# Keys and values lead the queries by eight tiles in the last layer, and the first new rows are gathered inside the projection

## The chip, the cores and the metric

The kernel runs on one core of a Trainium2 chip. The metric is the device time of one execution in microseconds (us), and a smaller time is better. Each engine of the core (TensorE or PE for matrix products, VectorE or DVE, ScalarE or ACT, GpSimd or POOL, and SyncE or SP, which issues transfers) takes its own list of instructions in order and waits for the others through semaphores.

## The reference

Four layers add to a residual x of 2048 tokens by 512 features. The first three (mixtures of experts, attention with low-rank projections, soft routing) are not touched. The last layer matters here:

```
# _L3_cond_ref, cut: new keys and values go into a paged cache, then window attention
q = x @ Wq.T; k = x @ Wk.T; v = x @ Wv.T     # 8 query heads, 4 key heads, 64 wide
q = _rms(q, q_norm_scale); k = _rms(k, k_norm_scale)
pos = kv_lens[:, None] + arange(Tx)
q = _rope(q, pos); k = _rope(k, pos)
k_blocks = k_blocks.at[blk, :, off, :].set(k)                 # and the same for v
allowed = (kpos <= pos) & (kpos > pos - 256)
p = softmax(where(allowed, q @ k_all.T / 16, -inf))
y = (p @ v_all) @ Wo.T
# _L3_ffn_ref: y is quantised to int8 by row, multiplied with an int8 weight, scaled, bias added
```

For each of the 32 sequences a window of the cache is attended to. Some of its rows are old (they come from the given cache), some are new (keys and values of this layer, from whichever sequence wrote to that block of the cache).

## The kernel before, in words

`layer3` works on 16 tiles of 128 tokens (`NT` = 16) in two stages.

**Projection.** A list `units` holds (1, i) for "keys and values of tile i" and (0, i) for "queries of tile i". It is built with `LAG` = 5: the queries of tile t − 5 follow the keys and values of tile t. So five key-and-value units come first, then the two kinds alternate, and after (1, 15) a few query units remain. The last `LAST` = 3 query tiles (13, 14, 15) are not in the list. The loop over u runs through the units and five steps more. In each step:

- `turn` transposes a tile of x on PE for the next kv unit and keeps the result for LAG + 3 = 8 tiles, since the queries use it later;
- four matmuls (L1852) multiply the tile with the weights into PSUM (`pp`);
- `l3_length` squares (ACT L1947), sums (DVE L1949) and takes the power −1/2 (POOL L1952);
- two steps later (one for the last kv tile) `l3_rotate` multiplies with the norm (DVE `n` L1964), with the cosine table (DVE `tc` L1970) and with the sine table (POOL `ts` L1970); one step after that its `add` (DVE L1979) finishes the rotation;
- a finished kv tile is stored to the DRAM buffer `newkv` (SP, L1879); a finished query tile is transposed five steps after its unit by `heads` (PE L1826, two ACT copies L1828 into `qT`);
- from u = 3 to 26 `old_rows` loads one of the first 24 cache tiles `kvt` from the old cache.

Query tiles i ≥ NT − LAG = 11 are `late`: they are only copied to `qlate` (ACT L1860) and normalised and rotated during attention, by the generator `queries`.

After the loop `new_rows(0)` and `new_rows(1)` gather new rows over the old ones: three indirect transfers each (POOL L284), which read `newkv` and so wait until all its stores have landed. They are kept in program order against one another.

**Attention.** A loop over s works in steps of one sequence and half of its heads: `keys` (PE transposes `kp` L2003, ACT copy `kT`), `scores` (PE `sp`, DVE, ACT exponential), `turn0`/`turn1` (PE `pT`), `values` (PE `op`), `product` (PE `y`). Its first steps also project the tiles 13 to 15 (`project`, PE L1910, ACT copy L1912) and call `new_rows(2)`, `new_rows(3)` and so on. A scheduler merges the instructions of the program into one list for each engine; only those that are pinned or kept in program order among themselves are not moved against one another.

Of the kernel before, what the change touches and what calls it, by code (L numbers as in the profile page):

```python
# [22 lines left out]
NT = B * T // P  # L23
# [1724 lines left out]
            yield  # L1748


LAG = 5
LAST = 3


def layer3(g, w, xs, xb):
# [3 lines left out]
    with ExitStack() as ctx:  # L1759
# [6 lines left out]
        def fetch(i):  # L1766
            if i < NT:
                x[i] = g.load_x(xp, xs, i, 4, later=True)
# [11 lines left out]
        def old_rows():  # L1780

            if not kvs or len(kvs[-1]) == 3:
                if len(kvs) == B:
                    return
                kvs.append([])
            t = cache.tile([CH, D], F32, name="kvt")
            g.dma(t, w["rows"][len(kvs) - 1, len(kvs[-1])])
            kvs[-1].append(t)

        def new_rows(b):  # L1790
            if b < B:
                for c in range(3):
                    col = c * B + b
                    g.gather(kvs[b][c], new, w["oidx"][0:CH, col : col + 1], bound=N - 1, later=True)

        with ExitStack() as c1:
            xp = c1.enter_context(tc.tile_pool(name="l3x", bufs=4, reuse_waits="tile"))
            for part in (slice(0, 4), slice(4, NT)):
                g.dma(tab[1][:, part], w["tab"][:, 1, part])
                fetch(2 if part.start == 0 else 3)  # L1800
            sb = c1.enter_context(tc.tile_pool(name="l3pj", bufs=2, reuse_waits="tile"))
            ps = c1.enter_context(tc.tile_pool(name="l3pq", bufs=3, space=PSUM, reuse_waits="tile"))
            units = [
                (z, i) for t in range(NT + LAG) for z, i in ((1, t), (0, t - LAG)) if 0 <= i < NT - (not z) * LAST
            ]

            lag = [1 if unit == (1, NT - 1) else 2 for unit in units]
            xT, held, turned = {}, [], {}

            def turn(i):  # L1810
                if i < NT - LAST:
                    xT[i] = g.transpose4(ps, sb, x[i], "xT3", bufs=3, keep=LAG + 3, pin=True)
                elif i < NT:

                    tp = ps.tile([P, 4, P], F32, name="tp", tag="tp", bufs=3)
                    for c in range(4):
                        g.first(c, nc.tensor.transpose(tp[:, c, :], x[i][:, c * P : (c + 1) * P], g.ident))
                    j = 4 * (i - NT + LAST)
                    xT[i] = tab[1][:, j : j + 4, :]
                    g.evac(xT[i], tp)  # L1820
                fetch(i + 4)

            def heads(ps, i, q):
                tp = ps.tile([P, 4, P], F32, name="tp", tag="tp", bufs=3)
                for c in range(4):
                    nc.tensor.transpose(tp[:, c, :], q[:, c * P : (c + 1) * P], g.ident)  # L1826
                for b in range(2):
                    nc.scalar.copy(  # L1828
                        qT[i][:, b], tp[:, :, 64 * b : 64 * b + 64].rearrange("p (a h) t -> p a h t", a=2)
                    )  # L1830

            slow = []
            turn(0)
            outs = []
            for u in range(len(units) + 5):
                if u == 1:
                    g.dma(wq, a["w_q3"])
                    g.dma(tab[0], w["tab"][:, 0])
                elif u == 12:
                    w["w_o3"] = g.load(wp, "w_o3", later=True)  # L1840
                    w["jt"] = g.load(wp, "jt", later=True)
                    for k in ("wqT", "wsb"):
                        t = wp.tile(list(w[k].shape), w[k].dtype, name=f"{k}3")
                        g.dma(t, w[k])
                        w[k] = t
                if u < len(units):
                    z, i = units[u]
                    if z:
                        turn(i + 1)
                    pp = ps.tile([P, D], F32, name="pp3", tag="pp", bufs=5)  # L1850
                    for c in range(4):
                        nc.tensor.matmul(  # L1852
                            pp, xT[i][:, c, :], (w["w_kv3"] if z else wq)[:, c, :], start=c == 0, stop=c == 3
                        )
                    late = not z and i >= NT - LAG
                    out = wp.tile([P, D], F32, name=f"qlate{i}") if late else sb.tile([P, D], F32, name="qkv3", bufs=6)
                    outs.append(out)
                    if late:

                        nc.scalar.copy(out, pp)  # L1860
                        slow.append((i, out))
                        held.append(None)
                    elif z:
                        nc.scalar.copy(out[:, 256:512], pp[:, 256:512])
                        held.append((pp, out, l3_length(g, sb, pp[:, 0:256])))
                    else:
                        held.append((pp, out, l3_length(g, sb, pp)))
                for k, (z, i) in enumerate(units[: u + 1]):
                    if not held[k]:
                        continue  # L1870
                    if u == k + lag[k]:
                        pp, out, r = held[k]
                        held[k] = l3_rotate(
                            g, sb, out[:, 0:256] if z else out, pp[:, 0:256] if z else pp, r, tab[z][:, i]
                        )
                    elif u == k + lag[k] + 1:
                        out = held[k]()
                        if z:
                            nc.sync.dma_start(out=new[i * P : (i + 1) * P, :], in_=outs[k])  # L1879
                        else:  # L1880
                            turned[k] = out
                if 3 <= u < 27:
                    old_rows()
                if u - 5 in turned:
                    heads(ps, units[u - 5][1], turned[u - 5])
            new_rows(0)
            new_rows(1)

        sb = pool("l3sb", 2)
        ps = pool("l3ps", 3, space=PSUM)  # L1890
# [51 lines left out]
def l3_length(g, sb, src, late=False):  # L1942

    nc = g.nc
    m = src.shape[1] // 64
    sq = sb.tile([P, m, 64], F32, name="sq3")
    nc.scalar.activation(sq, src.rearrange("p (h d) -> p h d", d=64), AF.Square)  # L1947
    ss = sb.tile([P, m], F32, name="ss3", bufs=3)
    nc.vector.tensor_reduce(ss, sq, AX.X, ALU.add)  # L1949
    nc.vector.tensor_scalar(ss, ss, 1.0 / 64, 1e-6, ALU.mult, ALU.add)  # L1950
    r = sb.tile([P, m], F32, name="r3", bufs=3)
    ins = nc.gpsimd.tensor_tensor(r, ss, g.c("nhalf")[:, 0:m], ALU.pow)  # L1952
    if late:
        g.pin(ins)
    return r


def l3_rotate(g, sb, out, src, r, tab):


    nc = g.nc
    m = src.shape[1] // 64
    n = sb.tile([P, m, 64], F32, name="n3")
    g.tc.keep_in_program_order(nc.vector.tensor_tensor(  # L1964
        n, src.rearrange("p (h d) -> p h d", d=64), r.unsqueeze(2).to_broadcast([P, m, 64]), ALU.mult
    ))
    tc_ = sb.tile([P, m, 2, 32], F32, name="tc3")
    ts = sb.tile([P, m, 2, 32], F32, name="ts3")
    for t, k, eng in ((ts, 1, nc.gpsimd), (tc_, 0, nc.vector)):
        eng.tensor_tensor(  # L1970
            t.rearrange("p h z d -> p h (z d)"), n,
            tab[:, 64 * k : 64 * k + 64].unsqueeze(1).to_broadcast([P, m, 64]), ALU.mult,
        )

    def add():
        o = out.rearrange("p (h z d) -> p h z d", z=2, d=32)
        for z, op in ((0, ALU.subtract), (1, ALU.add)):
            g.tc.keep_in_program_order(
                nc.vector.tensor_tensor(o[:, :, z, :], tc_[:, :, z, :], ts[:, :, 1 - z, :], op)  # L1979
            )  # L1980
        return out

    return add
# [178 lines left out]
```

## Time and profile before

| | us |
|---|---|
| median of three runs | 2708.14 (2706.84 to 2720.64) |
| the profiled execution | 2699.47 |
| its span in the trace | 2697.7 |
| mean granted TensorE clock | 0.969 of full |
| projection of the last layer | about 2284 to 2392 |
| attention at an even pace | from about 2434 |

How to read the profile: the page counts the busy time of each engine and the costliest groups of instructions by line, output and input. The timeline lists instructions of all engines by start, with length, engine, line, operation, output and input; in square brackets stands how long the engine had been idle before, and what ended this. The windows give the busy time of each engine in a stretch, with the number of instructions, the granted clock, the share of the transfer engines and what they moved in GB/s. The view of waits sums idle time by the instruction that waited and by what released it.

### The profile page before, as it was taken

To read this page: it belongs to the slowest core of one execution; us is meant where nothing else is said; L and a number is where in the kernel's file an instruction comes from. 1 tells how busy PE (TensorE), PEld (TensorE's weight loads), DVE (VectorE), ACT (ScalarE), POOL (GpSimd) and SP (SyncE) were. 2 spreads that over 40 slices of the span, in tenths; PEclk is the share of its full clock that TensorE was granted. 3 is DMA by queue.
4 is the path that set the end of the run, shared out by engine and by line. 5 is a ranking of instruction groups with operands and counts; after the bars stand their busy time and mean duration, and the time that the engine had idled before them with its cause. 6 is when DMAs were issued, how large, how long until landed. Compare 5 with 4: busy or idle time off the path is not lost.

```text
span 2697.7 us, 42340 instructions
## 1 busy us (share of the span) xinstructions
PE 2526.4 (94%) x16523; PEld 1623.4 (60%) x16523; DVE 1416.6 (53%) x3439; ACT 723.6 (27%) x1501; POOL 850.8 (32%) x904
## 2 busy tenths in 40 slices
PE   6999998996699999996899999999999999989998
PEld 5777775563565555564566666666666665435554
DVE  4666655643744444444444444555554431557886
ACT  2344430111311121010222222222222221236664
POOL 2222214623232233212222333233332321563440
PEclk9999999997699999997899999999999999999999
DMA  2333214445656976544222222222222222523441
GB/s 98 131 123 116 90 70 169 158 151 196 214 181 226 339 260 227 201 163 169 59 69 69 73 81 82 74 73 72 73 73 76 80 71 99 182 77 108 136 138 48
DMA packets 136213, 343.58 MB, mean 127 GB/s; under 512 B 24249, under 2 KB 25049, under 8 KB 128704
## 3 DMA queue, kind: packets, MB, share of 16 engines
q1 hardware_dynamic: 100368, 245.84, 26.4%
q0 software_dynamic: 35056, 89.13, 11.0%
q10 hardware_dynamic: 576, 5.77, 0.5%
q8 instruction: 134, 2.20, 0.3%
q14 instruction: 79, 0.65, 0.1%
HBM read 247.10 MB, written 109.58 MB: 132 GB/s over the span
## 4 chain that ended last, share of the span: by engine, by line
PE 43%; DVE 8%; issue 1%; DMA 1%; ACT 0%; POOL 0%; another core or an unknown queue 0%; SPq 0%; ACTq 0%; POOLq 0%; DVEq 0%
PE out L1539 8%; PE lp L1396 7%; PE pp L1852 3%; PE gp L1528 3%; PE zp L1473 3%; PE y L2099 2%; PE yp L1341 2%; PE op L2077 2%; PE pT L2052 2%; PE hp L1505 2%; PE sp L2030 2%; DVE xt L1025 1%; PE ep L1482 1%; DVE inv L1432 1%; PE kp L2003 1%
## 5 line engine op out<-in xcount | busy, mean ns | idle before, releaser
L943 PE MATMUL gu<-xT,wt 128*128 128x320 f32 x1472 | 407.8, 433 | 0.0
L943 PEld LDWEIGHTS gu<-xT,wt 128*128 128x128 f32 x1472 | 278.2, 191 | 123.1 <-issue 16.2
L1539 PE MATMUL out<-sb_w,gT 128*128 128x512 f32 x512 | 233.6, 599 | 11.1 <-DVE nn L1376 6.7
L1396 PEld LDWEIGHTS lp<-xnT,sb_mu 128*128 128x128 f32 x2048 | 236.1, 194 | 8.7 <-issue 6.7
L962 PE MATMUL y<-wt,hT 128*128 128x512 f32 (+1 forms) x552 | 239.4, 605 | 1.2 <-DVE yo L971 0.7
L1396 PE MATMUL lp<-xnT,sb_mu 128*128 128x128 f32 x2048 | 239.1, 277 | 1.5 <-DVE xnT L256 0.8
L1473 PE MATMUL zp<-sb_w,xnT 128*128 128x512 f32 x512 | 228.3, 595 | 2.7 <-DVE z L1475 2.6
L284 POOL DMA_INDIRECT kvst<-kv,gidx x96 | 96.8, 1009 | 264.4 <-DMA oldkv<-kvst 190.3
L1532 DVE COPY gT<-gp 128x512 f32<-128x512 f32 x64 | 44.3, 691 | 248.4 <-PE gp L1528 248.0
L1539 PEld LDWEIGHTS out<-sb_w,gT 128*128 128x128 f32 x512 | 93.4, 190 | 116.2 <-issue 95.2
L1473 PEld LDWEIGHTS zp<-sb_w,xnT 128*128 128x128 f32 x512 | 93.7, 190 | 110.5 <-issue 97.4
L284 POOL DMA_INDIRECT xr<-rows,stok x115 | 110.1, 957 | 150.2 <-PE tp L924 79.7
L962 PEld LDWEIGHTS y<-wt,hT 128*128 128x128 f32 (+1 forms) x552 | 80.3, 171 | 99.7 <-issue 83.1
L284 POOL DMA_INDIRECT kvt<-newkv,oidx x96 | 98.0, 1021 | 131.9 <-DMA kvt<-oldkv 99.1
L677 POOL TENSOR_TENSOR ga<-ga,sg 128x320 f32<-128x320 f32 x64 | 55.2, 862 | 265.5 <-ACT sg L673 265.5
L284 POOL DMA_INDIRECT yk<-ys,slot x96 | 97.6, 1016 | 126.3 <-SPq L823 65.3
L1510 ACT ACTIVATE h<-hp 128x512 f32<-128x512 f32 x128 | 69.5, 594 | 222.2 <-PE hp L1505 222.1
L673 ACT ACTIVATE sg<-ga 128x320 f32<-128x320 f32 x64 | 30.0, 469 | 277.1 <-DVE ga L671 271.1
L924 PEld LDWEIGHTS tp<-sb_cst,xr 128*128 128x128 f32 x460 | 53.5, 146 | 66.0 <-issue 40.1
L971 DVE TENSOR_TENSOR yo<-y,bd 128x512 f32<-128x512 f32 (+1 forms) x96 | 66.3, 690 | 50.8 <-PE y L962 47.2
L1434 POOL TENSOR_TENSOR eT<-eT,inv 128x512 f32<-128x512 f32 x64 | 71.9, 1125 | 64.9 <-DVE inv L1433 59.5
L1401 DVE TENSOR_TENSOR lT<-lp,cmu 128x512 f32<-128x512 f32 x64 | 43.5, 680 | 92.3 <-PE lp L1396 86.2
(379 smaller groups left out, 4558.1 us busy)
## 6 DMA issues: line engine op xcount, KB each, us to landing
wt<-w_e SPq DMA_DIRECT2D x32, 1538.0 KB
ys<-yo SPq DMA_DIRECT2D x115, 256.0 KB
oldkv<-kvst SPq DMA_DIRECT2D x96, 224.0 KB
kvt<-oldkv SPq DMA_DIRECT2D x96, 224.0 KB
ys<-zero SPq DMA_DIRECT2D x10, 2048.0 KB
xt<-x SPq DMA_DIRECT2D x62, 256.0 KB
x<-xt SPq DMA_DIRECT2D x48, 256.0 KB
wt<-w_e SPq DMA_DIRECT2D x7, 1536.0 KB
```

Source lines behind the costliest of these rows:

```text
L284: ins = self.nc.gpsimd.indirect_dma_start(out=out, out_offset=None, in_=src, in_offset=bass.IndirectOffsetOnAxis(ap=idx, axis=0), **kw)
L677: nc.gpsimd.tensor_tensor(ga, ga, sg, ALU.mult)
L943: nc.tensor.matmul(o, wj[:, c, ic * P : (ic + 1) * P], xT[:, c, :], start=c == 0, stop=c == 3)
L962: nc.tensor.matmul(y[row : row + n, :], hTs[u][:, ic, col : col + n], wd[:, ic, :], start=ic == 0, stop=ic == 1,)
L971: nc.vector.tensor_tensor(yo[r], y[r], bd[r], ALU.add)
L1396: g.first(e + c, nc.tensor.matmul(lp[:, e, :], w["mu"][:, c, (4 * q + e) * P : (4 * q + e + 1) * P], self.xnT[:, c, :], start=c == 0, stop ...
L1434: g.pin(nc.gpsimd.tensor_tensor(e3, e3, inv.unsqueeze(2).to_broadcast([P, 8, T]), ALU.mult))
L1473: g.first(c, nc.tensor.matmul(zp, self.xnT[:, c, :], w["w1"][:, c, cols], start=c == 0, stop=c == 3))
L1510: g.pin(nc.scalar.activation(self.hs[q][b], hp[:, b], AF.Gelu))
L1528: g.first(e + b + k, nc.tensor.matmul(gp[r, e, cols], self.hs[q][b][:, e, r], self.lT[q][:, e, cols], start=True, stop=True))
L1539: g.first(e, nc.tensor.matmul(self.out, self.gTs[q][:, e, :], w["w2"][:, 4 * q + e, :], start=q + e == 0, stop=q + e == 6 and q == 3))
L1852: nc.tensor.matmul(pp, xT[i][:, c, :], (w["w_kv3"] if z else wq)[:, c, :], start=c == 0, stop=c == 3)
```

## The change

The queries now follow the keys and values at a distance of eight tiles. The transposed x tiles are kept for 11 tiles instead of 8, because `keep` is LAG + 3. A constant of its own, `LATE` = 5, keeps the set of late query tiles as it was (11 and 12 in the list). The list has 29 units as before; the unit (1, 15) is number 22 in it instead of 25. The calls of `new_rows(0)` and `new_rows(1)`, which stood after the loop, now stand in the loop, three and four steps after that unit, which is u = 25 and u = 26. `new_rows(2)` and the following ones are called where they were.

```diff
-LAG = 5
+LAG = 8
+LATE = 5
 LAST = 3
...
-                    late = not z and i >= NT - LAG
+                    late = not z and i >= NT - LATE
...
                 if 3 <= u < 27:
                     old_rows()
+
+                if u - units.index((1, NT - 1)) in (3, 4):
+                    new_rows(u - units.index((1, NT - 1)) - 3)
                 if u - 5 in turned:
                     heads(ps, units[u - 5][1], turned[u - 5])
-            new_rows(0)
-            new_rows(1)
```

## The prediction

> **What bounds the kernel now.** I read four views, in this order: the page (who is busy), the windows around the stage the change touches, the timeline of its end, and the waits there.
>
> ```profile
> PE 2526.4 (94%) x16523; PEld 1623.4 (60%) x16523; DVE 1416.6 (53%) x3439; ACT 723.6 (27%) x1501; POOL 850.8 (32%) x904
> ...
> L284 POOL DMA_INDIRECT kvt<-newkv,oidx x96 | 98.0, 1021 | 131.9 <-DMA kvt<-oldkv 99.1
> ```
>
> TensorE is busy 94% of the span, so a change that only moves work can gain only where it stands still. The 96 gathers that fetch new rows cost POOL about 1 us each, a tenth of its busy time. Next the windows (us, then busy time of PE, PEld, DVE, ACT, POOL, then the clock):
>
> ```profile
> 2300.00:2350.00 50.00, 50.00 (x147) 24.07 (x147) 30.46 (x83) 11.25 (x29) 29.17 (x27) 1.00 0.54 185
> 2350.00:2400.00 50.00, 47.76 (x141) 23.16 (x140) 31.98 (x79) 16.82 (x43) 32.49 (x29) 0.97 0.33 108
> 2400.00:2425.00 25.00, 14.54 (x56) 6.89 (x55) 7.24 (x25) 9.51 (x21) 19.61 (x20) 0.89 0.17 44
> 2425.00:2450.00 25.00, 24.28 (x160) 14.33 (x162) 19.07 (x70) 16.23 (x49) 9.11 (x9) 0.84 0.27 74
> ```
>
> The projection is solid TensorE until about 2392; the hole is the passage into attention, where PE is busy 14.5 of 25 us. The timeline shows what fills the passage:
>
> ```profile
> 2377.68 3.60 PE L1852 MATMUL pp<-w_kv,tab 128*128 128x512 f32 x8
> ...
> 2388.86 3.60 PE L1852 MATMUL pp<-w_q,xT 128*128 128x512 f32 x8
> ...
> 2391.62 0.34 SPq L1879 DMA_DIRECT2D newkv<-qkv  x1
> ...
> 2392.31 1.27 POOL L1970 TENSOR_TENSOR ts<-n,tab 128x512 f32<-128x512 f32 x1 [1.76 <-DVE n L1964]
> ...
> 2394.43 1.22 POOL L284 DMA_INDIRECT kvt<-newkv,oidx  x1 [0.85 <-DMA xt<-x2b]
> ...
> 2395.13 0.73 PE L1826 MATMUL tp<-sb_cst,qkv 128*128 128x128 f32 x4 [2.24 <-DVE qkv L1979]
> 2395.65 5.24 PE L1910 MATMUL pp<-w_q,tab 128*128 128x512 f32 x8
> ...
> 2404.43 0.32 PE L2003 MATMUL kp<-sb_cst,kvt 112*128 112x112 f32 x1 [1.25 <-DMA kvt<-newkv,oidx]
> ...
> 2417.66 1.67 POOL L1952 TENSOR_TENSOR r<-ss,sb_cst 128x8 f32<-128x8 f32 x1
> ...
> 2421.92 0.82 PE L2003 MATMUL kp<-sb_cst,kvt 112*128 112x112 f32 x3 [7.48 <-ACT qlate L1912]
> ...
> 2434.22 0.51 PE L2003 MATMUL kp<-sb_cst,kvt 112*128 112x112 f32 x3
> ```
>
> The last key-and-value tile (kv15) is multiplied at 2377.68, its rows are stored at 2391.62, the first gather follows 2.8 us later, and eighteen gathers at one per 1.28 us hold POOL to 2417.6. The power (L1952) of query 11 stands behind them. The waits of 2390 to 2432 give its price:
>
> ```profile
> PE kp L2003 <- ACT qlate L1912: 7.5, 1, 7.5
> ...
> DVE ss L1949 <- POOL r L1952: 6.7, 1, 6.7
> ...
> PE kp L2003 <- DMA kvt<-newkv,oidx: 1.8, 2, 1.2
> ```
>
> The gathers' landing, which the change brings forward, cost PE only 1.8 us; their occupation of POOL costs more: DVE stops 6.7 us and PE 7.5 us.
>
> **What the Trainium skill says.** "TensorE: Matmul & The Clock Gate", What's actually happening: the array runs at half or full clock, watched in windows of about 3.4 us; an idle window halves it. The trace agrees: granted clock is 0.5 from 2395.5 to 2398.9 and from 2419.4 to 2433.1, and eight matmuls that take 3.60 us take 5.24 at 2395.65. The same page (Architectural detail) calls the GpSimd queue strict first in, first out; the trace agrees, query 11's power starting only after gather eighteen. "DMA: Bandwidth & Descriptors", Anatomy of one DMA: about 2 us fixed, mostly the receipt of the write. The trace has 2.8 us from the store's issue to the gather; I use 2.8.
>
> **The change part by part.** In the compiled order the instructions are the same ones; only places differ.
>
> *Where kv15 goes.* After it come six query units instead of three. A query unit takes 3.44 us on PE, a head's transposes 0.44. Query 12 ends at 2391.4 (before 2392.3: two transposes now stand after it). So kv15 ends at 2391.4 − 6×3.44 − 3×0.44 = 2369.5, instead of 2381.1. Store after the same 10.6 us: 2380.1; first gather 2.8 later: 2382.95, 11.5 us earlier. SP issues the stores in order, each just when its tile is ready, and the x loads were issued at least 10 us ahead, so neither queue pays. The other end of the stage (eight kv units ahead instead of five) is costed at nothing: a kv unit needs of POOL 1.12+0.88 us and of DVE about 2, under PE's 3.9. If an x tile came late there, PE would wait for it; three tiles brought forward by 3.4 us each bound that at 10 us.
>
> *POOL's new order.* This is what the diff doesn't show. Only six gathers are written into the loop, but the scheduler lets later ones pass the queries' rotations (ts, 1.27 us) too: gather, power q9, gather, ts q7, 3 gathers, power q10, gather, ts q8, 3 gathers, ts q9, 2 gathers, ts q10, 7 gathers, power q11, 6 gathers. With 1.28 per gather, 1.64 per power and 1.27 per ts, from 2382.95: ts q7 ends 2388.4, ts q8 2396.5, ts q9 2401.7, ts q10 2405.5, gather eighteen 2414.4, power q11 2416.1, the last gather 2423.7 (before 2427.0). Before, ts q10 ended 2393.6, ahead of every gather.
>
> *What that does to PE.* PE is in order and each head's transposes wait for ts plus DVE's add (0.76). The transposes of q8, q9, q10 come at 2397.3, 2402.5, 2406.4 instead of 2388.4, 2392.3, 2395.1. Project13 stands behind them: 2406.9 instead of 2395.65, **11.2 us later**. PE is nearly idle from 2392 to 2406, so the clock is halved and project13 takes 5.24 again, to about 2412.4.
>
> *What is given back.* Before, the stretch from the end of project13 (2400.9) to the kp of 2421.92 took 21.0 us. Gone from it are (a) the two gather waits, 1.8, since the first nine rows land early; (b) the stall on query 11's power, 7.5: it is ready at 2416.1, while DVE needs it only after project14 (2414.4 to 2417.9) and the copy and square of its result (0.6 each), at about 2419. ACT has one square more than before behind the last head copy (six masks and two late queries, 4.3 us, until 2412.5); the first key copy then comes at once, beside project14: nothing. So this kp comes at 2412.4 + 21.0 − 9.3 = 2424.1, 2.2 late. (c) The idle of 2414 to 2422 brought the half clock of 2419.4 to 2433.1, under which two attention steps took 2434.22 − 2421.92 = 12.3 us. Without the idle they run at full clock. From 2434.22 on such a step takes 3.67 us with the output product beside it; these two have none yet. PE was busy 10.3 of the 12.3 us, which is 5.2 at full clock, and two steps of 3.67 are 7.3; I take 5.8 to 6.8. The kp of 2434.22 thus comes at 2429.9 to 2430.9. **Net: 3.4 to 4.3 us earlier, I take 4.** From there the loop is the same work at its own pace.
>
> The profiled execution took 2699.47 us with a span of 2697.7; it becomes 2695.5. The median of the runs is 2708.14, 8.7 above the profiled one; I carry the difference over: **2704 us**.
>
> Unknown costs, from both sides: gathers beside DVE work, 1.22 (the first) to 1.5 us, which for the ten before ts q10 means −0.6 to +2.2; the two steps after it 5.2 to 12.3 (taken 6.3), that is −1 to +6; project13 at full clock −1.6, at half 0 (taken); key copies behind ACT's squares 0 (taken) to +1.5; an x tile late at the start 0 (taken) to +10.
>
> **Rivals.** *Forecast:* delay 11 us, returned in the passage: 2704.
> *Faster:* POOL gets through the mixed order sooner (the heads late by about 5 us instead of 11) and PE stays warm. The passage holds 21.3 us of PE work at full clock in 41.9 us, so 20.6 is all that can be won; with 5 us lost (the six gathers written into the loop, 7.7, less POOL's slack of 1.0 per query unit over three units) kp comes at 2392.3+21.3+5 = 2418.6, 15.6 earlier: 2692.5. For it: first gather 11.5 us earlier and the power stall gone. Against it: ten gathers stand ahead of ts q10, 12.8 us that cannot be overlapped in a first-in queue.
> *Slower:* the heads of q8 to q10 wait behind gathers and the old stall isn't returned, only moved: with before's 38.6 us from project13 to kp at 2434.22 unchanged, the end is 2406.9+38.6 = 2445.5, 11.3 later; each microsecond that ts q10 is later than 2405.5 adds one. With gathers at 1.5 (+2.2) and ACT's +1.5 it is +15: 2723. It decides when ts q10 ends after 2407.7 and DVE still waits for query 11's power. For it: every link is in order. Against it: the power has 3 us to spare.
> *Gathers don't move in effect:* the first gather waits for all stores and an older load (0.85 <-DMA xt in before); if this keeps it at 2394, ts q7 to q10 stand behind that wait too and project13 is later by up to 11.5 us more: 2704 + 11.5 = 2715, a loss with the same sign as the slower rival. Against it: the loads concerned were issued long before.
>
> **How the numbers follow.** What a measurement of this kernel can tell from no change is 0.5%, 13.5 us. Forecast 0.62 (its own range 2695 to 2715), faster rival 0.14, slower 0.17, late gather 0.07. The range takes in the forecast's bounds and part of both sides: 2690 to 2722. Faster than 2694.6: 0.15. Slower than 2721.7: 0.20. Between: 0.65.
>
> **What would show it.** First gather near 2383; ts q10 (POOL L1970) near 2404 to 2406; PE idle before the transposes at L1826 about 4 to 6 us each for q8 and q9, 3 for q10; project13 at 2406 to 2408 at half clock; no wait of DVE ss on POOL r; the 7.5 us of kp on qlate gone; clock full by 2420. Wrong, if PE shows no idle before L1826 (then faster), or if a wait of 6 us or more stands after 2412 (then slower).

## The result and the profile after

On the chip of the prediction the changed kernel took 2703.29 us (median of 14 runs, 2695.53 to 2717.24) against 2711.03 us before (14 runs, 2706.23 to 2720.64). The ratio is 0.9973, 95% interval 0.9962 to 0.9983: about 7 us less, where the prediction had called anything under 13.5 us no change.

The time of a whole run hides where this came from, so times below are also given against the start of the last layer's projection, its first key-and-value matmul; "+127" means 127 us after it. In the profiled run of before this start is at 2281.87, after it is at 2288.09: everything ahead of it, which the change doesn't touch, took 6.2 us longer in the second execution. That is why the profiled execution after has a span of 2703.5 us and yet no slower last layer.

First the windows of the changed kernel (us, busy time of PE, PEld, DVE, ACT, POOL, clock, share of the transfer engines, GB/s):

```profile
2350.00:2400.00 50.00, 48.23 (x140) 22.91 (x138) 29.77 (x73) 12.57 (x33) 34.28 (x28) 1.00 0.29 91
2400.00:2425.00 25.00, 12.64 (x39) 6.83 (x40) 9.07 (x21) 8.48 (x20) 21.31 (x19) 0.66 0.27 69
2425.00:2450.00 25.00, 25.00 (x168) 14.09 (x168) 19.92 (x78) 20.32 (x59) 9.97 (x10) 1.00 0.27 76
```

The hole is about as large as before (12.6 busy us of 25, before 14.5), but it lies earlier in the stage, which stands 6.2 us later in this trace. Its clock is lower (0.66, before 0.89), and the stretch after it is full at full clock (25.00 busy, clock 1.00; before 24.28 at 0.84). Next the timeline of TensorE and POOL in the hole (start, length, engine, line, operation; in brackets the idle time before it and its end):

```profile
2389.51 1.40 POOL L284 DMA_INDIRECT kvt<-newkv,oidx  x1 [2.36 <-DMA kvt<-oldkv]
...
2402.36 1.27 POOL L1972 TENSOR_TENSOR ts<-n,tab 128x512 f32<-128x512 f32 x1
...
2404.57 1.09 PE L1827 MATMUL tp<-sb_cst,qkv 128*128 128x128 f32 x4 [6.34 <-DVE qkv L1981]
...
2410.11 1.09 PE L1827 MATMUL tp<-sb_cst,qkv 128*128 128x128 f32 x4 [4.46 <-DVE qkv L1981]
...
2412.16 1.28 POOL L1972 TENSOR_TENSOR ts<-n,tab 128x512 f32<-128x512 f32 x1
...
2414.38 1.08 PE L1827 MATMUL tp<-sb_cst,qkv 128*128 128x128 f32 x4 [3.18 <-DVE qkv L1981]
2415.26 5.57 PE L1912 MATMUL pp<-w_q,tab 128*128 128x512 f32 x8
...
2422.51 1.67 POOL L1954 TENSOR_TENSOR r<-ss,sb_cst 128x8 f32<-128x8 f32 x1
...
2437.97 0.51 PE L2005 MATMUL kp<-sb_cst,kvt 112*128 112x112 f32 x3
```

The three heads of q8, q9 and q10 wait 6.34, 4.46 and 3.18 us, 14.0 in sum, each for DVE's add, and this for a sine product (POOL L1972) that stands among gathers. Project13 starts at 2415.26, which is +127.2 (before +113.8), at half clock. From there nothing stalls. The waits from 2370 to 2440 say it in one view:

```profile
DVE qkv L1981 <- POOL ts L1972: 15.2, 4, 6.4
PE tp L1827 <- DVE qkv L1981: 14.0, 3, 6.3
...
POOL kvt L284 <- DMA kvt<-oldkv: 2.4, 1, 2.4
```

No line "DVE ss <- POOL r" and no "PE kp <- ACT qlate" is left in this stretch; they were 6.7 and 7.5 us. The seventh key transposes, which ended the passage before at 2434.22 (+152.35), come at 2437.97 (+149.88), 2.5 us earlier.

### The profile page after: what moved, and what is told of

Read it like the earlier page. It is cut to its first block, busy times and chain, and to the rows that moved or that the text cites. A ratio compares the mean times of both kernels' runs of the same rounds, so it can differ in the third digit from the quotient of the medians.

```text
span 2703.5 us, 42331 instructions
## 1 busy us (share of the span) xinstructions
PE 2524.2 (93%) x16508; PEld 1622.9 (60%) x16523; DVE 1416.7 (52%) x3439; ACT 721.4 (27%) x1501; POOL 854.1 (32%) x904
## 4 chain that ended last, share of the span: by engine, by line
PE 42%; DVE 9%; issue 1%; POOL 1%; DMA 1%; ACT 0%; another core or an unknown queue 0%; SPq 0%; ACTq 0%; POOLq 0%; DVEq 0%
PE out L1539 8%; PE lp L1396 7%; PE gp L1528 3%; PE zp L1473 3%; PE pp L1853 3%; PE yp L1341 2%; PE y L2101 2%; PE hp L1505 2%; PE op L2079 2%; PE pT L2054 2%; PE sp L2032 2%; DVE xt L1025 1%; PE ep L1482 1%; DVE inv L1432 1%; PE kp L2005 1%
## 5 line engine op out<-in xcount | busy, mean ns | idle before, releaser
L284 POOL DMA_INDIRECT yk<-ys,slot x96 | 98.6, 1027 | 125.4 <-DVE adf L1159 65.2
```

The source lines that it names most:

```text
L284: ins = self.nc.gpsimd.indirect_dma_start(out=out, out_offset=None, in_=src, in_offset=bass.IndirectOffsetOnAxis(ap=idx, axis=0), **kw)
```

## The experiments

They ran on three more occasions, each with runs of the kernel before on the same chip (three different chips). Its median was 2660.7 us in the first (e1 to e4), 2712.7 in the second (e5 to e8) and 2659.5 in the third (e9 to e12); it had been 2711.0 at the prediction. There are thus two groups of chips, about 50 us apart, and this turned out to matter. Each of the three was used on one occasion only, so the runs don't tell a matter of the chip from one of the occasion; where the text says chip, it can be either. Positions against the stage's start, from one profiled execution each:

| kernel | chip, before's median | ratio to before (95%) | project13 | seventh keys | last output |
|---|---|---|---|---|---|
| before | 2711 | 1 | +113.8 | +152.4 | +412.4 |
| changed | 2711 | 0.9973 (0.9962 to 0.9983) | +127.2 | +149.9 | +412.0 |
| e1 gathers only | 2661 | 1.0002 (0.9993 to 1.0011) | +114.3 | +146.5 | +404.0 |
| e2 lead only | 2661 | 1.0011 (1.0003 to 1.0019) | +127.1 | +150.0 | +406.1 |
| e3 before, six buffers | 2661 | 0.9966 (0.9954 to 0.9978) | +114.3 | +140.5 | +394.0 |
| e4 later gathers held back | 2661 | 1.0005 (0.9997 to 1.0013) | +123.9 | +148.0 | +405.6 |
| e5 changed again | 2713 | 0.9985 (0.9976 to 0.9994) | +127.2 | +149.7 | +413.4 |
| e6 sines on VectorE | 2713 | 0.9989 (0.9979 to 1.0000) | +117.6 | +150.4 | +414.7 |
| e7 changed, six buffers | 2713 | 0.9965 (0.9952 to 0.9978) | +127.2 | +150.4 | +412.0 |
| e8 before, six buffers, early projections | 2713 | 1.0002 (0.9989 to 1.0015) | in the loop | +155.4 | +420.4 |
| e9 before again | 2660 | 1.0004 (0.9994 to 1.0013) | +114.3 | +146.2 | +403.7 |
| e10 lead of six, six buffers | 2660 | 0.9967 (0.9955 to 0.9980) | +116.0 | +139.4 | +394.5 |
| e11 sines on VectorE, six buffers | 2660 | 0.9976 (0.9967 to 0.9985) | +117.5 | +140.3 | +394.3 |
| e12 as e3 | 2660 | 0.9966 (0.9953 to 0.9979) | +113.8 | +138.5 | +392.6 |

**e1 and e2: the two halves of the change.** Against the changed kernel, e1 takes the lead back and e2 the early call of the gathers:

```diff
 e1
-LAG = 8
+LAG = 5
 e2
-                if u - units.index((1, NT - 1)) in (3, 4):
-                    new_rows(u - units.index((1, NT - 1)) - 3)
...
+            new_rows(0)
+            new_rows(1)
```

> LAG stays 5; only the first two groups of gathers are called inside the loop, three and four steps after the last key-and-value unit. If the change works through the order of the units (theory A), this alone does nothing: ratio to before 0.999 to 1.001, passage from the end of query 12 to the seventh key transposes about 42 us as before, first gather right after query 10's rotation, 18 gathers in a row, the 7 us stop of DVE on query 11's power still there. If the early call of the gathers is what brings the gain (theory B), ratio about 0.997 and the passage is shorter by 2 us or more.

> LAG 8 with LATE 5, but the gathers called after the loop as before. Theory A: the same as the changed kernel, ratio to before about 0.997, first gather about 11 us earlier against the stage's start, heads of q8 to q10 late by 4 to 6 us each, passage about 40 us. Theory B: no gain, ratio 0.999 to 1.001.

Measured: 1.0002 and 1.0011. In the compiled program every engine's list of e1 equals that of before, instruction by instruction, and e2's equals that of the changed kernel: the scheduler put the gathers in the same places, whichever of the two steps of the program called them. So the half of the change that moves the calls does nothing, and theory B is out: what is left is the lead of eight tiles. The positions of e2 are the changed kernel's through the whole passage (+101.4 for the first gather, waits of 6.34, 4.46 and 3.18 us, the seventh keys at +150.0 where the changed kernel had +149.9). But its ratio isn't: on this chip the same lists are 0.1% slower than before. The difference is on before's side. Here its passage is 5.9 us shorter (seventh keys at +146.5 instead of +152.4), so that the same changed passage is 2.5 us shorter than before's on one chip and 3.5 us longer on the other. The seventh keys of e1 and e2, whose stages start at 2252.47 and 2256.82:

```profile
2398.97 0.51 PE L2005 MATMUL kp<-sb_cst,kvt 112*128 112x112 f32 x3
...
2406.79 0.51 PE L2004 MATMUL kp<-sb_cst,kvt 112*128 112x112 f32 x3
```

At the last output 2.1 of the 3.5 us are left in the pair of traces; the medians of e2 and of before on this chip differ by 3.6 us (2664.26 and 2660.70).

**e3: the wait on query 11's power.**

```diff
-    ss = sb.tile([P, m], F32, name="ss3", bufs=3)
+    ss = sb.tile([P, m], F32, name="ss3", bufs=6 if late else 3)
...
-    r = sb.tile([P, m], F32, name="r3", bufs=3)
+    r = sb.tile([P, m], F32, name="r3", bufs=6 if late else 3)
```

> The kernel before, with six instead of three buffers for the sums and powers of the late queries, so that the fourth late sum no longer waits for query 11's power behind eighteen gathers. If that power is what held PE at 2414 to 2422 (theory A), the 6.7 us wait of DVE and the 7.5 us wait of PE go, the half clock after them too: passage 30 to 34 us instead of 42, ratio 0.9955 to 0.9975. If the gathers' landing or something else held it (rival), the wait only changes its name: passage 40 us or more, ratio 0.999 to 1.001.

Measured: 0.9966, as theory A had it. On this chip before (the list of e1, 2362 to 2405) waits like this:

```profile
DVE ss L1951 <- POOL r L1954: 7.9, 1, 7.9
...
PE sp L2032 <- DVE m L2039: 5.6, 1, 5.6
```

Both lines are gone in e3, and its seventh keys come 6.0 us earlier. The order on POOL is unchanged; the fourth sum of the late queries no longer needs a buffer that the power of the first still reads. (With the buffers free, the scheduler also placed some instructions of VectorE and ScalarE differently; what that alone does was not measured.) Another 2.6 us were gained later, between +164 and +192, and the same waits from 2405 on show why. They hold one more such line in e1, and none in e3:

```profile
DVE ss L1951 <- POOL r L1954: 3.9, 1, 3.9
```

It is the sum of query 15, which needed the buffer of query 12's power, and this stands behind the next gathers. I had not seen it in the forecast; it is there in before and in the changed kernel alike.

**e4: later gathers held back.** The indices of gathers seven to nine are copied behind project13's result, those of the next fifteen behind project15's:

```diff
+        def gate(b0, b1, src):
+            n = b1 - b0
+            t = wp.tile([P, 3 * n], I32, name=f"oidx{b0}")
+            nc.vector.tensor_copy(t[0:1, 0:1], src[0:1, 0:1])
+            nc.vector.tensor_copy(
+                t.rearrange("p (c b) -> p c b", b=n), w["oidx"].rearrange("p (c b) -> p c b", b=B)[:, :, b0:b1]
+            )
...
+            if i != NT - 2:
+                gate(*((2, 3) if i < NT - 2 else (3, 8)), out)
```

Six late buffers as in e3.

> The changed kernel, in which the third group of gathers waits for project13's result and the groups four to eight for project15's (through a copy of their indices), so that POOL does the sine products of q8 to q10 before them; the late sums have six buffers. Theory A (heads were late because their sine products stood behind gathers): heads of q8, q9 come with at most 3 us of idle before them, project13 starts 6 to 10 us earlier against query 12's end than in the changed kernel, passage 28 to 34 us, ratio to before 0.994 to 0.997. Rival (the heads wait for DVE or ACT, not for POOL): project13 no earlier than in the changed kernel, passage 38 us or more.

Measured: 1.0005, project13 only 3.2 us earlier than in e2, passage 38.3 us. Neither expectation held whole (the passage is as the rival had it, project13 is not), and the waits (2360 to 2410) say why:

```profile
POOL kvt L284 <- DVE oidx L1797: 14.3, 2, 8.0
...
PE tp L1839 <- DVE qkv L1998: 10.7, 3, 6.4
```

The gate was too late: POOL now stands idle for 14.3 us and the rows come late. And the head of q8 still waits 6.35 us, since six gathers and two powers are ahead of its sine product without the hoisted ones. Only q9 and q10 profit (2.16 us each instead of 4.46 and 3.18). So the six early gathers carry nearly half of the delay. Since the gate brought a wait of its own, the time of this kernel decides nothing between the two expectations.

**e5: the changed kernel again**, on a chip where before takes 2713 us.

> The changed kernel itself. If its gain is a property of the program (theory A), ratio to before again about 0.997, and the seventh key transposes come about 2.5 us earlier against the stage's start than in before. If the first comparison caught a pause of TensorE in the passage that belongs to the chip it ran on and not to the program (theory C, from e2, whose instruction lists are the changed kernel's), ratio 1.000 to 1.002, and the seventh key transposes come 0 to 1.5 us later.

Measured: 0.9985, between the two expectations. The seventh keys come at +149.7, as in the first run (+149.9) and in e2 (+150.0). So the changed kernel's passage is the same on both groups of chips, and only before's differs, by 5.9 us.

**e6: no head behind a gather.** The sine products of q8 to q10 go to VectorE:

```diff
-    for t, k, eng in ((ts, 1, nc.gpsimd), (tc_, 0, nc.vector)):
+    for t, k, eng in ((ts, 1, sine or nc.gpsimd), (tc_, 0, nc.vector)):
...
+                            nc.vector if not z and i >= 8 else None,
```

> The changed kernel with the sine products of q8, q9 and q10 on VectorE instead of POOL, so that no head stands behind gathers; all else as it is. If the gathers on POOL delay the heads (theory A), the three waits of 6.3, 4.5 and 3.2 us shrink to below 6 us in sum, project13 starts near +116 to +119 after the stage's start instead of +127; part of it is lost again on query 11's power behind 24 gathers (wait of DVE 2 to 8 us); ratio to before 0.996 to 1.000. If the heads wait for DVE's own queue (rival), project13 stays at +124 or later and the ratio at 1.001.

Measured: waits of 0.58, 2.10 and 1.89 us in place of 6.34, 4.46 and 3.18; project13 at +117.6, ten us earlier, as theory A had it. The rival is out: the heads waited for POOL. The wait on query 11's power that it also expected did not come. Yet the seventh keys come no earlier (+150.4), and the ratio is 0.9989. What took the ten us shows in its waits (2395 to 2450):

```profile
DVE s L2040 <- remote: 9.4, 3, 8.1
ACT qlate L1915 <- remote: 8.0, 1, 8.0
...
PE tp L1827 <- DVE qkv L1982: 4.6, 3, 2.1
```

The last line is the sum of the three waits of the heads. "Remote" stands where the profile shows no own engine or transfer that ended the wait. ACT waits here for project14's matmuls, whose records end 8 us before the wait does. The same line stood in the trace of before that I predicted from (waits of 2390 to 2432); there it was project15's matmuls, and their records had ended 8 us before too:

```profile
ACT qlate L1912 <- remote: 8.6, 1, 8.6
```

No trace from the 2660 us chips has a wait put down to "remote" anywhere. I call it the pause below.

**e7: both halves of e3 in the changed kernel.** The edit is e3's.

> The changed kernel with six buffers for the late sums and powers. If the change only trades the wait on query 11's power for late heads (theory A), the extra buffers find no wait left to remove: same as the changed kernel, ratio to before 1.000 to 1.002 where e3 (before with six buffers) had 0.9966, so with these buffers the change is a loss of 0.3 to 0.5%. If the buffers help in another way than by that wait (rival), the ratio falls below 0.998 here too.

Measured: 0.9965, so by the ratio the rival. By the trace it is both: the passage is unchanged (seventh keys +150.4, e5 +149.7), since there is no wait on query 11's power left to remove; then 2.8 us are gained between +168 and +196, where the 3.9 us wait of query 15's sum is gone. The traces differ by 1.4 us in all, the medians by 5.8; the rest isn't explained.

**e8: projections ahead of the heads.** Query tiles 13 to 15 enter the list of units and leave the attention loop; LAG 5, six buffers:

```diff
-                (z, i) for t in range(NT + LAG) for z, i in ((1, t), (0, t - LAG)) if 0 <= i < NT - (not z) * LAST
+                (z, i) for t in range(NT + LAG) for z, i in ((1, t), (0, t - LAG)) if 0 <= i < NT
...
-            if s == -3:
-                project(NT - LAST)
...
-            if -3 < s < LAST - 3:
-                project(NT - LAST + s + 3)
```

> The kernel before (LAG 5) with six buffers, and with the query tiles 13 to 15 projected in the loop of units, ahead of the last heads, instead of among the first keys. If TensorE in the passage lacks ready work and loses its clock (theory A), the 10.4 us of matmuls cover the heads' 2.2 us and the landing of the first gathers, the clock stays full: passage 25 to 29 us, ratio 0.9945 to 0.9965. If the gathers' rate of one per 1.28 us is what the first attention steps wait for (rival), the keys wait for rows instead and the ratio stays at 0.9966 as in e3.

Measured: 1.0002, the seventh keys at +155.4. Neither theory: the waits (2395 to 2450) hold the same sign as e6, in a worse form.

```profile
DVE s L2033 <- remote: 11.9, 2, 7.7
...
PE sp L2026 <- issue: 10.4, 2, 7.5
```

TensorE stands still for 7.5 us while it waits for nothing that the profile shows. Whether the early projections pay on the 2660 us chips wasn't tried.

**e9 to e12**, all on a chip of the 2660 us group. e10 is the changed kernel with LAG = 6 and e3's buffers, e11 the edits of e6 and e3 together, e12 is e3.

> The kernel before itself, with a second trace. Ratio 0.9995 to 1.0005. Theory C (on some chips TensorE's results reach the others late in this passage, and only the order before is hit by it): on a chip where the changed kernel is at 0.998 or below, the trace shows again a wait of ACT or DVE of 6 us or more put down to remote between +128 and +140 us after the stage's start, and the seventh key transposes near +152; on a chip like that of e1 to e4 it shows none, and they are near +146.5. Rival: the pause was chance, and the trace shows none on any chip.

> LAG 6 with LATE 5 and six late buffers: the last key-and-value unit moves by one query unit, 3.9 us, and in POOL's order three gathers stand ahead of query 10's sine product and none ahead of q8's and q9's. If the harm comes from gathers ahead of the heads (theory A), project13 starts 1 to 3 us later than in e3 (+114.3) where LAG 8 had 13, the gather waits of 1.8 us go, and the ratio to before is that of e12 (e3's kernel) within 0.0015. If a larger lead is harmful or good in itself (rival), it lies a third of the way from e12 to e7.

> LAG 8 with both waits taken away: the sine products of q8 to q10 on VectorE, six late buffers. If the late heads and the waits on late powers are all that LAG 8 pays (theory A), it is at least as fast as e12: project13 near +117, passage 28 to 34 us on a chip without the pause, ratio to before 0.994 to 0.997. If early gathers are worth nothing (rival, the transfers were hidden before), it is not faster than e12: 0.996 to 0.998.

> The kernel of e3 on the chip of e9 to e11: 0.9955 to 0.9975 again, 6 us of it in the passage and 2.5 us in the loop where the sum of query tile 15 waited for query 12's power; if its gain were a matter of the chip, 0.998 to 1.000.

e9: no pause, the seventh keys at +146.2. The passage of before is now known on two such chips (+146.5, +146.2), but on one of the 2711 us group only from the trace of the prediction. e10: project13 at +116.0, the gather waits gone, the seventh keys at +139.4 (e12 +138.5), 0.9967 against 0.9966 for e12: a lead of six costs and gains nothing. e11: with both waits removed the lead of eight is at 0.9976, passage 30.4 us (e12 27.9), so it isn't faster than the lead of five. This is the rival's case: the rows that come 11 us earlier were not missed. e12 repeats e3.

## Why the prediction was right, point by point

The forecast of 2704 us and of no change beyond 0.5% held: 2703.29. That the two times agree so closely is partly luck: the forecast took off 4 us from a median of 2708.14, while the 14 runs have 7.7 us between 2711.03 and 2703.29. That the passage became shorter at all is luck in the same sense: it rests on a wait that the forecast took for another, as the last step below shows. Of the steps:

- *kv15 and the first gather.* Held: +101.4 after the stage's start, forecast 2382.95, which is +101.1. The reason was a little other than said: by the profile gather one didn't wait last for a store but 2.36 us for an old row's load, and in before for an x load. So no trace here shows what the landing of a store costs, and the 2.8 us that were carried over are no measure of it.
- *POOL's order and the late heads.* Held, mis-sized by 2 us. The sine product of q10 was forecast to end at +123.6 and ended at 2413.44, +125.4; project13 was forecast at +125.0 and started at +127.2. Term by term: forecast delay 11.2 us, measured 13.4. From the first gather to the end of q10's sine product are 23.9 us; without the powers and sine products 15.5 are left, 1.41 us for each of eleven gathers, idle time included, where the forecast had 1.28. Some of them last up to 1.40 us instead of 0.98; why isn't shown. (The forecast's list has eleven gathers there too, though its text counts ten, and its end of project13 should be 2412.1 by its own numbers, not 2412.4.) e6 and e11 confirm the cause: without POOL in the heads' way project13 is ten us earlier.
- *Half clock during project13.* Held: 5.57 us (forecast 5.24). The trace has the clock at half from +114 to +131.
- *The gather waits and the stall on the power, 9.3 us given back.* Held in the trace of the changed kernel: neither is left. That query 11's power holds PE is shown by e3 on the 2660 us chips, at 6.0 us in the passage there (e12 against e9: 7.7). In before's trace from the prediction's chip, though, the 7.5 us of PE ended with the ACT copy that waited for "remote", not with the sum on DVE. I had counted as one stall what on that chip was a stall and a pause at the same time.
- *The two steps at full clock.* Held: 2432.40 to 2437.97 is 5.6 us, forecast 5.8 to 6.8.
- *Net 4 us earlier.* Measured 2.5 in the passage, from a delay of 13.4 us of project13 and 15.9 us given back (forecast 11.2 and 15.2). On the 2660 us chips the same lists (e2 against e1) delay project13 by 12.8 us and give back 9.3, so the passage is 3.5 us longer. The delay is there as forecast; what is missing is part of the return. Before has no pause to lose there: in e1 its PE stands 5.6 us for the power instead of 7.5, and the half clock that begins then lasts 6.8 us instead of 13.7. So there the mechanism of the forecast makes the passage longer, and the sign on the prediction's chip goes with the pause that I had not seen as one (before's trace there is the only one of its kind).

Only the passage is accounted for in this way. The gain of 7 us on the prediction's chip is more than its pair of traces shows (2.5 us at the seventh keys, 0.4 us at the last output). The profiled execution of before took 2699.47 us, less than any of the 14 timed ones (2706.23 at least), so this one trace may not be typical of before, and where the rest of the gain lies is open. Why the pause costs the changed kernel nothing (e5 has 2.5 us of it in the passage and comes at +149.7 all the same) is open too. A TensorE that stands 14 us before the heads anyway may hide it; e6 and e8, which don't stand there, were hit by it again. This is argued from six traces on such chips and not shown. What the pause is stays open, as does whether it comes in every execution of before there.

The best version measured on the 2660 us chips is e3's edit alone: on the kernel before it gives 0.9966 twice, on two chips. On the other group it was run only in the changed kernel (e7, 0.9965) and together with the early projections (e8, 1.0002), so whether it is enough by itself there is not known.

## What to carry to other kernels

When transfers are issued from an engine that also computes, starting them earlier puts them ahead of that engine's other work. Count what stands behind them in its compiled order before counting what they bring, and check whether anybody missed the data: here 1.8 us did. Look also for the small buffer that chains two engines: three more buffers of 32 bytes per partition for each of two small tiles, which let a sum run ahead of a queued power, were worth more on the 2660 us chips than the new order of the whole stage (0.9966 against 1.0011). And compare positions on a second chip before calling a wait a property of the program: part of the stall that the forecast counted on was not there on the other chips.

## What the runs showed of the hardware

The chips fall into two groups: the same kernel takes about 2660 us on one and 2711 on the other. All six traces from the 2711 us group have waits put down to "remote" (the longest is 21.4 us on ScalarE, in e5; in the passage it is 8.6 us, in before); the eight from the other have none at all. Whether this is the cause of the 50 us isn't shown. A part of a per cent that is measured on one chip can have the other sign on the next: 0.9973 and 0.9985 on the 2711 us group, 1.0011 on the 2660 us one, for the same instruction lists.
